# Woven stages of a four-layer convolution network: the frames' shift moved into the statistics, other pauses in the plan, one product per sample in the last layer

## The chip, the cores and the metric

The kernel is one program on one core of a Trainium2 chip. The metric is the time of one execution on the device in microseconds (us). Engines are named as in the profile: PE is TensorE (PEld its loads of weights), DVE is VectorE, ACT is ScalarE, POOL is GpSimd, SP is the engine that issues nearly all DMAs. L584 is line 584 of the kernel.

## The reference

The input x has shape (16, 32, 128, 128), 16 samples b of 32 channels. Four layers follow one another, each of the form x + f(gn(x)), where gn normalises groups of two channels of a sample:

```python
x = x + _L0_conv_ref(_gn(x), ...)   # a row LSTM: scan over 128 columns, two small products per step
x = x + _L1_conv_ref(_gn(x), ...)   # AdderNet: out = -sum over 32 channels and 3x3 taps of |patch - w|
x = x + _L2_conv_ref(_gn(x), ...)   # Hartley transform, 32x32 modes mixed over channels, transform back
x = x + _L3_conv_ref(_gn(x), ...)   # U-net: 5 edge operators, each normalised; 3x3 convs, max-pools,
                                    # 2x2 deconvs; its result multiplies the normalised input
```

The last line is `x + xn * y` with xn the normalised input and y the U-net's output, that is (x - mean) * (1 + istd * y) + mean.

## The kernel before

**Layer 0** (`stage0`, to some 920 us) runs alone; the change does not touch it.

**Layers 1 to 3** are in `rest`. Layer 1 is the class `Differences`. For each of 16 samples and two halves it makes 72 tensors of max(q - w, 0), one per tap and filter group (d_dve on VectorE at L681, 2.36 us; d_act on ScalarE at L678, 7.15 us), and PE sums each with 16 products (L584). Every half ends with `finish` (L567, L569). The quantised input q of the next half is loaded with one DMA of 2145 KB (L553, `q<-q_d`), whose source is read as [4 copies, 32 channels, 66 rows].

Layers 2 and 3 are the class `After`, one generator over groups of four samples. Groups 0, 1 and 2 are woven into layer 1 (the woven stage, to some 6130 us); group 3, and what is left of group 2, run when layer 1 is done (the drain). A group goes through, in this order:

- `forward`: loads xh (L957), products with the transform (L1026, L996), modes exchanged through memory, then `mixing`: 32 rows ky of 16 small products (L1092) with weights `mix` in eight pieces of four rows, three buffers, each piece loaded (L1079) when the piece three before it is used; the result is copied (L1107) and stored.
- `back`: loads zi, products (L1153), then 16 steps n: eight products (L1198) for step n, a pause, and `take_out` of step n - 1 (L1176 adds to the rows xr, L1178 their statistics). Rows are stored (L1182) and the buffer of four is reloaded (L1132) for step n + 4. Then the mean and istd of the group (`bn_aggr` at L1214, `normalised`) go into `stats3`.
- `frames`: loads rows of layer 3's input (L1237) and normalises them on ScalarE (L1248), with scale istd and bias -mean * istd (the shift, `fr_shift`, L1245). They are used by `statistics` (L1288, then es_w at L1348) and by `conv1` (L1603). Between these the weights wf are made from the statistics (L1413, L1415), then the edge sums cut (L1575).
- `small_layers` (L1451, L819), and `last`: per unit and row parity pr, the last composed convolution (L819), s = istd * acc + (1 + istd * bias) (L1730), the multiply (x - mean) * s (L1695), plus mean on ScalarE (L1703), store (L1709).

**The plan.** The order of instructions on each engine is fixed when the program is built, by `Weave`. It keeps planned times for DVE, ACT and PE. After each tap of layer 1, `advance` takes steps of the chain while PE's planned time is less than some 2 us ahead of the time at which the next tap ends. A generator's `yield 1.1` is 1.1 us of PE work; `yield -7.0` is a pause: the chain goes on when the planned time is 7.0 us later; `later(us, step)` puts a step off by so much. A pause puts no wait into the program: it only decides which of layer 1's instructions stand between. The core of it is

```python
elif v < 0:
    wait = -v
...
if wait > 0:
    self.until = self.now + wait
```

In the drain two such generators are stepped in turn, the one with the smaller planned time first. A group starts when its four samples of layer 1 are planned (`("after", 4 * g + 3)`) and the group before has ended.

Of the kernel before, what the change touches and what calls it, by code (L numbers as in the profile page):

```python
# [7 lines left out]
F32 = mybir.dt.float32  # L8
F16 = mybir.dt.float16
I32 = mybir.dt.int32  # L10
AF = mybir.ActivationFunctionType
ALU = mybir.AluOpType
# [3 lines left out]
B, C, H, W = 16, 32, 128, 128  # L16
# [3 lines left out]
M1 = 32  # L20
# [23 lines left out]
def bc_view(t, g):  # L44

    return t.rearrange("b c h w -> (b c) (h w)")[g * 128 : (g + 1) * 128]
# [826 lines left out]
class After:  # L873
# [13 lines left out]
    def work(self, groups):  # L887
        if 0 in groups:
            yield from self.prepare()
        for g in groups:  # L890
            with self.pool("g_sm") as sm:
                yield ("after", 4 * g + 3)
                yield -8.0
                self.stats3 = sm.tile([128, 2, 1], F32, name="stats3")
                yield from self.forward(g)
                with ExitStack() as kept:
                    yield from self.encoder(g, kept)
                    yield from self.last(g)
# [183 lines left out]
    def mixing(self, g, xs, wp, wt):  # L1082


        nc, weave, z_d = self.nc, self.weave, self.d["z"]
        zp = [self.acc() for _ in range(2)]
        zv = [z.rearrange("p (y k b) -> p y k b", k=4, b=8) for z in zp]
        for ky in range(M1):
            w = wt[ky // 4]
            for k in range(16):  # L1090
                j = k // 4
                nc.tensor.matmul(  # L1092
                    zv[ky // 16][32 * j : 32 * j + 32, ky % 16, k % 4, :],
                    w[:, ky % 4, k, :],
                    xs[:, :, k, ky],
                    start=True,
                    stop=True,
                )
            if ky % 4 == 3 and len(wt) < M1 // 4:
                wt.append(self.weights(wp, len(wt)))  # L1100
            yield 1.1
        yield SUMMED
        zs = wp.tile([128, 2, 4, 4, 32], F32, name="zs", bufs=1)
        for half in range(2):
            for y in range(2):
                dst = zs[:, half, :, :, 16 * y : 16 * y + 16].rearrange("p b k y -> p y k b")
                nc.vector.tensor_copy(dst, zv[y][:, :, :, 4 * half : 4 * half + 4])  # L1107
        weave.dve += 2.0
        yield -2.5
        for half in range(2):  # L1110
            for j in range(4):
                first = z_d.offset + 4 * g * 32768 + 512 * half + 128 * j
                dst = bass.AP(z_d.tensor, first, [[1024, 32], [32768, 4], [1, 128]])
                nc.sync.dma_start(dst, zs[32 * j : 32 * j + 32, half].rearrange("p b k y -> p b (k y)"))
        yield -4.0

    def back(self, g, load):


        nc, tc, cst, d, weave = self.nc, self.tc, self.cst, self.d, self.weave  # L1120
        x2, x3, z_d = d["x2"], d["x3"], d["z"]

        with self.pool("t_z") as zp_, self.pool("t_r", 4) as rp:
# [68 lines left out]
            for n in range(16):  # L1192
                s, half = n // 2, n % 2
                pf = [self.acc() for _ in range(2)]
                for i in range(4):
                    for r in range(2):
                        part = slice(64 * half + 32 * r, 64 * half + 32 * r + 32)
                        nc.tensor.matmul(  # L1198
                            pf[r][:, W * i : W * i + W],
                            o1[part, 4 * s + i].rearrange("p b o -> p (b o)"),  # L1200
                            cst["cas_t"][part, :],
                            start=True,
                            stop=True,
                        )
                yield 0.8
                if previous:
                    yield -7.0
                    take_out(*previous)
                previous = n, pf
            yield SUMMED  # L1210
# [2 lines left out]
            mv = zp_.tile([128, 1, 2], F32, name="mv3")  # L1213
            nc.vector.bn_aggr(mv[:, 0, :], stat.rearrange("p a b -> p (a b)"))  # L1214
            yield from normalised(nc, zp_, self.ps, weave, mv, 1, cst["avg2_bc"], 1e-5, self.stats3)

    def frames(self, g, pool):

        nc, x3, weave = self.nc, self.d["x3"], self.weave
        shift = []
        ring = [pool.tile([128, 20, W + 4], F32, name=f"xp{i}") for i in range(2)]
        for t in ring:
            nc.vector.memset(t[:, :, 0], 0.0)
            nc.vector.memset(t[:, :, W + 3], 0.0)

        def parts(ch, half):

            lo, hi = max(16 * ch - 2 + 10 * half, 0), min(16 * ch + 8 + 10 * half, H)
            off = lo - (16 * ch - 2)
            return ring[ch % 2], lo, hi, ring[ch % 2][:, off : off + hi - lo, 2 : W + 2]

        def load(ch, half):
            t, lo, hi, v = parts(ch, half)
            nc.sync.dma_start(v, bc_view(x3, g).rearrange("p (h w) -> p h w", w=W)[:, lo:hi, :])  # L1237

        def normalise(ch, half, us):
            t, lo, hi, v = parts(ch, half)  # L1240

            def step():
                if not shift:
                    shift.append(pool.tile([128, 1], F32, name="fr_shift"))
                    nc.vector.scalar_tensor_tensor(  # L1245
                        shift[0], self.stats3[:, 0], -1.0, self.stats3[:, 1], ALU.mult, ALU.mult
                    )
                nc.scalar.activation(v, v, AF.Identity, bias=shift[0], scale=self.stats3[:, 1])  # L1248
                for edge, r, src, zero in ((lo == 0, 1, 3, 0), (hi == H, 18, 16, 19)):
                    if edge:  # L1250
                        nc.gpsimd.memset(t[:, zero, :], 0.0)
                        nc.scalar.copy(t[:, r, 2 : W + 2], t[:, src, 2 : W + 2])
                own = slice(10 * half, 10 * half + 10)
                nc.scalar.copy(t[:, own, 1], t[:, own, 3])
                nc.scalar.copy(t[:, own, W + 2], t[:, own, W])
                weave.act += 2.0

            return weave.later(us, step)

        chunk = lambda ch: ring[ch % 2]  # L1260
        return load, normalise, chunk

    def statistics(self, g, pool, frames, sides, out, tables):


# [393 lines left out]
    def last(self, g):  # L1659

        nc, tc, cst, weave = self.nc, self.tc, self.cst, self.weave
        with self.pool("l_y") as yp, self.pool("l_x", 2) as xp:
# [18 lines left out]
            p = self.acc()  # L1681
# [4 lines left out]
            mean, istd = ms[:, 0:4], ms[:, 4:8]  # L1686
# [3 lines left out]
            yield -4.0  # L1690

            def multiply(x, s, pr, blk):
                for pc in range(2):
                    v = x[:, blk].rearrange("p (r a w b) -> p r a w b", a=2, b=2, w=64)[:, :, pr, :, pc]
                    nc.vector.scalar_tensor_tensor(v, v, mean[:, blk : blk + 1], s[:, pc], ALU.subtract, ALU.mult)  # L1695
                weave.dve += 1.0


            following = {}
# [16 lines left out]
            def complete(unit):  # L1716
                while following.get(unit):
                    weave.done(following[unit])

            for unit in range(4):  # L1720
                complete(unit - 2)
                x = xr[unit % 2]
                for pr in range(2):
                    acc = [self.acc() for _ in range(4)]
                    for pc in range(2):
                        yield from up.round(y6, 64, acc, lambda j: (2 * pr + pc, 16 * unit + 4 * j, 4, 256 * pc))
                    yield SUMMED
                    for blk in range(4):
                        s = yp.tile([128, 2, 4, 64], F32, name="s", bufs=3)
                        nc.vector.tensor_scalar(  # L1730
                            s.rearrange("p b r w -> p (b r w)"),
                            acc[blk],
                            istd[:, blk : blk + 1],
                            one[:, blk : blk + 1],
                            ALU.mult,
                            ALU.add,
                        )
                        weave.dve += 0.65
                        if blk:
                            multiply(x, previous, pr, blk - 1)  # L1740
                        previous = s
                    multiply(x, previous, pr, 3)
                    yield -2.5
                following[unit] = weave.on_act(lambda x=x, unit=unit: done(x, unit))
            yield -36.0
            for unit in range(4):
                complete(unit)

# [160 lines left out]
```

## Time and profile before

| what | value |
|---|---|
| three timed runs | 7451.15, 7454.95, 7469.55 us (median 7454.95) |
| the profiled execution | span 7432.4 us, TensorE clock granted 0.86 |
| busy over the span | PE 75%, DVE 79%, ACT 71%, POOL 0% |
| d_dve (L681) | 1711 times, 2361 ns each |
| d_act (L678) | 593 times, 7146 ns each |
| last sum of layer 1 (L584) | 6129.4 us |
| group 0: mixing, rows of the way back, last wf, conv1 | from 2268, from 2461, to 2871, from 2903 us |
| group 1: xh, mixing, rows | from 3785, from 3975, from 4162 us |
| group 2: xh, mixing, rows, conv1, end | from 5495, 5689, 5873, 6341, to 7028 us |

The busy shares are means over stages with different limits, so the profile is read by stretches of time. A bracket such as [18.48 <-PE acc L584] at a row of the timeline says how long the engine was idle before it and what released it. A row with a count (x21) merges neighbours of one kind, and its second column is their length together.

### The profile page before, as it was taken

The page shows a single profiled execution, that of the slowest core. Times are in us where ns is not written, and L with a number is a line of the kernel's source. Part 1 is how long each engine was busy: PE and PEld are TensorE (multiplying, and loading weights), DVE is VectorE, ACT ScalarE, POOL GpSimd, SP SyncE. Part 2 cuts the span into 40 slices and gives each one's busy share as a digit, 9 for nine tenths or more (in the row PEclk, how much of TensorE's full clock was granted, in tenths as well). Part 3 has the DMA queues.
Part 4 walks back from the last instruction along what each step waited for, and adds up shares of the span by engine and source line. Part 5 has one row for each costly group of instructions (what it writes and reads, how often), then busy time and mean ns, then how long its engine had stood idle before and what let it go on. Part 6 is the DMA issues. An engine that isn't in the chain of part 4 may idle for free. (4 is left out here: it accounts for less than half of the span.)

```text
span 7432.4 us, 258307 instructions
## 1 busy us (share of the span) xinstructions
PE 5602.5 (75%) x121132; PEld 3087.2 (42%) x121132; DVE 5881.6 (79%) x7180; ACT 5276.7 (71%) x3110; POOL 34.2 (0%) x31
## 2 busy tenths in 40 slices
PE   4888466666676777998777676998777775898897
PEld 3666232222244343333344343333335345554554
DVE  7787599999988989999898988998898994135223
ACT  2556398889987988898898888898887980122222
POOL 0000000000000000000000000000000000000000
PEclk9899788888878888999888887998888885897996
DMA  8655111111033333111433332221343234244314
GB/s 314 225 183 172 61 64 54 46 53 52 33 95 95 119 110 96 57 53 46 98 108 103 102 111 94 63 67 42 75 113 108 82 117 144 65 141 119 80 30 95
DMA packets 374270, 721.68 MB, mean 97 GB/s; under 512 B 50896, under 2 KB 219856, under 8 KB 362320
## 3 DMA queue, kind: packets, MB, share of 16 engines
q1 hardware_dynamic: 372768, 704.58, 31.0%
q8 instruction: 948, 15.53, 0.9%
q14 instruction: 122, 1.00, 0.0%
q10 hardware_dynamic: 432, 0.57, 0.0%
HBM read 507.21 MB, written 164.32 MB: 90 GB/s over the span
## 5 line engine op out<-in xcount | busy, mean ns | idle before, releaser
L678 ACT ACTIVATE d_act<-q,neg 128x8192 f16<-128x8192 f16 (+1 forms) x593 | 4199.2, 7146 | 559.1 <-PE acc L584 512.6
L681 DVE TENSOR_SCALAR d_dve<-q,qw 128x8192 f16<-128x8192 f16 (+1 forms) x1711 | 3941.9, 2361 | 348.3 <-PE acc L584 306.1
L584 PE MATMUL acc<-d_dve,sel 128*32 128x512 f16 x27376 | 1963.3, 416 | 747.7 <-DVE d_dve L681 734.5
L584 PEld LDWEIGHTS <-sel 128*32 128x32 f16 x36864 | 1078.8, 103 | 2405.6 <-issue 1816.9
L1603 PE MATMUL acc<-xp,wf 32*32 32x512 f32 x25600 | 1014.7, 620 | 30.6 <-issue 15.2
L584 PE MATMUL acc<-d_act,sel 128*32 128x512 f16 x9488 | 738.6, 438 | 256.1 <-ACT d_act L678 244.0
L1603 PEld LDWEIGHTS acc<-xp,wf 32*32 32x32 f32 x25600 | 443.5, 105 | 404.4 <-issue 299.4
L1542 ACT ACTIVATE y<-pooled,b 32x128 f32<-32x128 f32 x512 | 204.7, 400 | 519.2 <-DVE pooled L1528 510.4
L819 PE MATMUL acc<-y,u_conv 32*32 32x256 f32 (+1 forms) x9728 | 443.3, 515 | 87.4 <-DVE s L1730 39.5
L207 PE MATMUL pg<-h,wb 64*64 64x20 f32 (+15 forms) x4096 | 403.1, 324 | 95.3 <-DVE h L256 54.1
L207 PE MATMUL pg<-e,wb 64*64 64x20 f32 (+15 forms) x4096 | 360.4, 320 | 16.0 <-DVE e L260 4.3
L244 ACT ACTIVATE gt<-pg,bias 128x20 f32<-128x20 f32 (+15 forms) x1024 | 315.5, 374 | 78.1 <-PE pg L207 70.9
L1248 ACT ACTIVATE xp<-xp,fr_shift,stats 128x1280 f32<-128x1280 f32 (+1 forms) x128 | 182.8, 1434 | 230.1 <-DMA xp<-x_d 174.2
L207 PEld LDWEIGHTS pg<-h,wb 64*64 64x64 f32 x4096 | 251.1, 156 | 131.0 <-DVE h L256 80.7
L819 PEld LDWEIGHTS acc<-y,u_conv 32*32 32x32 f32 x9728 | 199.7, 119 | 252.0 <-issue 155.4
L207 PE MATMUL pg<-xn,wb 64*64 64x28 f32 (+61 forms) x4096 | 291.1, 308 | 10.7 <-ACT gt L244 3.3
L207 PEld LDWEIGHTS pg<-e,wb 64*64 64x64 f32 x4096 | 256.1, 158 | 94.0 <-DVE e L260 65.8
L600 PE MATMUL acc<-q,sel 32*32 32x512 f16 x4608 | 151.8, 532 | 148.1 <-DVE xr L567 99.1
L1703 ACT ACTIVATE xr<-xr,l_ms 128x1024 f32<-128x1024 f32 x64 | 69.9, 1140 | 267.1 <-DVE xr L1695 267.1
L255 ACT ACTIVATE th<-c 128x20 f32<-128x20 f32 (+15 forms) x256 | 81.3, 320 | 239.7 <-DVE c L253 238.2
L1288 PE MATMUL acc<-xp 32*64 32x204 f32 (+3 forms) x8576 | 233.2, 343 | 13.5 <-issue 13.5
L207 PEld LDWEIGHTS pg<-xn,wb 64*64 64x64 f32 x4096 | 222.5, 157 | 35.7 <-ACT gt L244 8.3
(203 smaller groups left out, 4215.5 us busy)
## 6 DMA issues: line engine op xcount, KB each, us to landing
xr<-x_d SPq DMA_DIRECT2D x192, 512.0 KB
xp<-x_d SPq DMA_DIRECT2D x112, 640.0 KB
q<-q_d SPq DMA_DIRECT2D x32, 2145.0 KB
x_d<-xr SPq DMA_DIRECT2D x128, 512.0 KB
x_in<-in_x_dram SPq DMA_DIRECT2D x16, 2048.0 KB
res<-in_x_dram SPq DMA_DIRECT2D x64, 512.0 KB
xn<-in_xs_dram SPq DMA_DIRECT2D x64, 512.0 KB
xn<-xn SPq DMA_DIRECT2D x128, 256.0 KB
```

Source lines behind the costliest of these rows:

```text
L207: nc.tensor.matmul(bank[c][q][64 * pair : 64 * pair + 64, :, :width], wb[half, 4 * kind + KIND[q]].rearrange("p b o -> p (b o)"), v[half], ...
L244: nc.scalar.activation(gt[:, q, :, :n], bank[c][q][:, :, :n], AF.Tanh if q == G else AF.Sigmoid, bias=bias[:, KIND[q] : KIND[q] + 1],)
L255: nc.scalar.activation(th[:, :, :n], cell, AF.Tanh)
L584: self.nc.tensor.matmul(acc[k][32 * j : 32 * j + 32, :], self.sel16[:, i // 9, :], d[:, row : row + 4, c : c + W], start=False, stop=last,)
L600: self.nc.tensor.matmul(acc[k][32 * j : 32 * j + 32, :], self.sel16[rows, 8, :], q[rows, row : row + 4, kw : kw + W], start=tap == 0, stop ...
L678: nc.scalar.activation(dst, src, AF.Relu, bias=self.neg[:, i : i + 1])
L681: nc.vector.tensor_scalar(dst, src, self.qw[:, i : i + 1], 0.0, ALU.subtract, ALU.max)
L819: nc.tensor.matmul(acc[blk][32 * j : 32 * j + 32, o : o + rows * n], t[part, 4 * par + tap, :], src[part, top : top + rows, left : left + ...
L1248: nc.scalar.activation(v, v, AF.Identity, bias=shift[0], scale=self.stats3[:, 1])
L1288: nc.tensor.matmul(gram[blk][j : j + width, at : at + n], xp[part, l, 2 + j : 2 + j + width], xp[part, rows, j : j + width + 4], start=sta ...
L1542: nc.scalar.activation(d, s, AF.Identity, bias=bj)
L1603: nc.tensor.matmul(acc[blk][32 * j : 32 * j + 32, :], tap_of("all", tap)[rows], xp[rows, 4 * j + kh : 4 * j + kh + 4, kw : kw + W], start= ...
```

## The change

It makes the shift once, straight after the statistics of `back`, in a tile of the group, with a pause behind it; the frames then only use it. In `mixing` the planned price of a row is 1.0 instead of 1.1, and after rows 11, 15, 19, 23 and 27 there is a pause of 5.0. The pause before each `take_out` goes from 7.0 to 4.5. In `last` the two multiplies per sample, one for even and one for odd columns, become one over all columns; for it s is written with the two column parities interleaved. The pause at a group's end goes from 36 to 16.

```diff
+                self.shift3 = sm.tile([128, 1], F32, name="shift3")
...
                 wt.append(self.weights(wp, len(wt)))
-            yield 1.1
+            yield 1.0
+            if ky % 4 == 3 and 8 < ky < M1 - 1:
+                yield -5.0
...
                 if previous:
-                    yield -7.0
+                    yield -4.5
                     take_out(*previous)
...
             yield from normalised(nc, zp_, self.ps, weave, mv, 1, cst["avg2_bc"], 1e-5, self.stats3)
+            nc.vector.scalar_tensor_tensor(
+                self.shift3, self.stats3[:, 0], -1.0, self.stats3[:, 1], ALU.mult, ALU.mult
+            )
+            yield -2.5
...
             def step():
-                if not shift:
-                    shift.append(pool.tile([128, 1], F32, name="fr_shift"))
-                    nc.vector.scalar_tensor_tensor(
-                        shift[0], self.stats3[:, 0], -1.0, self.stats3[:, 1], ALU.mult, ALU.mult
-                    )
-                nc.scalar.activation(v, v, AF.Identity, bias=shift[0], scale=self.stats3[:, 1])
+                nc.scalar.activation(v, v, AF.Identity, bias=self.shift3, scale=self.stats3[:, 1])
...
             def multiply(x, s, pr, blk):
-                for pc in range(2):
-                    v = x[:, blk].rearrange("p (r a w b) -> p r a w b", a=2, b=2, w=64)[:, :, pr, :, pc]
-                    nc.vector.scalar_tensor_tensor(v, v, mean[:, blk : blk + 1], s[:, pc], ALU.subtract, ALU.mult)
-                weave.dve += 1.0
+                v = x[:, blk].rearrange("p (r a w) -> p a r w", a=2, w=W)[:, pr]
+                nc.vector.scalar_tensor_tensor(
+                    v, v, mean[:, blk : blk + 1], s.rearrange("p r w b -> p r (w b)"), ALU.subtract, ALU.mult
+                )
+                weave.dve += 0.7
...
-                        s = yp.tile([128, 2, 4, 64], F32, name="s", bufs=3)
+                        s = yp.tile([128, 4, 64, 2], F32, name="s", bufs=3)
                         nc.vector.tensor_scalar(
-                            s.rearrange("p b r w -> p (b r w)"),
-                            acc[blk],
+                            s.rearrange("p r w b -> p b r w"),
+                            acc[blk].rearrange("p (b r w) -> p b r w", b=2, w=64),
...
-            yield -36.0
+            yield -16.0
```

## The prediction

> **What bounds the kernel now.** I read the busy time in stretches first, cut where the last sum of layer 1 stands (6130 us), where group 2's first conv1 product stands (6341) and where group 2 ends (7028):
>
> ```profile
> core 0: us, PE busy (x) PEld busy (x) DVE busy (x) ACT busy (x) POOL busy (x), PEclk, DMA share, GB/s
> 923.00:6130.00 5207.00, 3918.91 (x79458) 1911.08 (x79450) 4788.49 (x3908) 4569.62 (x1245) 26.92 (x16) 0.87 0.27 81
> 6130.00:6341.00 211.00, 116.61 (x2384) 111.35 (x2369) 91.29 (x208) 12.54 (x23) 3.81 (x3) 0.56 0.46 138
> 6341.00:7028.00 687.00, 601.26 (x18232) 367.12 (x18239) 220.91 (x569) 166.54 (x320) 0.88 (x4) 0.88 0.37 101
> 7028.00:7432.00 404.00, 339.54 (x8660) 211.81 (x8645) 103.11 (x279) 92.49 (x169) 0.21 (x1) 0.78 0.28 65
> ```
>
> In the woven stage VectorE is busy 92% and ScalarE 88%: they bound it, and PE has room. In the drain PE bounds it, but for its first 211 us, where PE is busy 55% at a clock of 0.56. There group 2 is in a serial piece (statistics, es_w, wf) while group 3 starts.
>
> Then the idle time. The timeline of single engines has one stall of each kind per group or two:
>
> ```profile
> 2311.82 1.16 PE L1092 MATMUL acc<-xs,mix 128*32 128x8 f32 x29 [21.13 <-DMA mix<-in_mix_dram]
> 2314.89 47.88 DVE L681 TENSOR_SCALAR d_dve<-q,qw 128x8320 f16<-128x8320 f16 x21 [18.48 <-PE acc L584]
> 4018.43 2.39 DVE L681 TENSOR_SCALAR d_dve<-q,qw 128x8320 f16<-128x8320 f16 x1 [15.43 <-PE acc L584]
> 5730.75 2.39 DVE L681 TENSOR_SCALAR d_dve<-q,qw 128x8320 f16<-128x8320 f16 x1 [14.25 <-PE acc L584]
> ...
> 2627.24 1.29 DVE L1176 SCALAR_TENSOR_TENSOR xr<-acc,xr 128x512 f32<-128x512 f32 x2 [14.95 <-issue]
> 4324.92 1.29 DVE L1176 SCALAR_TENSOR_TENSOR xr<-acc,xr 128x512 f32<-128x512 f32 x2 [12.24 <-DMA xr<-x_d]
> ...
> 2647.13 1.25 ACT L1248 ACTIVATE xp<-xp,fr_shift,stats 128x1024 f32<-128x1024 f32 x1 [19.50 <-DVE fr_shift L1245]
> ```
>
> A mixing product waits for its weights, the sums of layer 1 stand behind it on PE, and VectorE runs out of buffers: 18.5 + 15.4 + 14.3 = 48 us. A take_out waits for its reloaded rows: 15.0 + 12.2 = 27 us. SP's timeline tells why:
>
> ```profile
> 2255.45 2.56 SPq L553 DMA_DIRECT2D q<-q_d  x1
> 2274.11 52.43 SPq L1079 DMA_DIRECT2D mix<-in_mix_dram  x5
> ...
> 4284.29 0.55 SPq L553 DMA_DIRECT2D q<-q_d  x1
> 4288.34 0.36 SPq L1132 DMA_DIRECT2D xr<-x_d  x1
> ```
>
> Each time the 2145 KB load of q was issued shortly before. Weights issued at 2274.1 held their product until 2311.8; a reload issued at 4288.3 held its take_out until 4324.9: some 37 us, against a 512 KB reload in about 4 us when nothing is in front (135 GB/s in 2540 to 2544).
>
> Last the chain of waits at the drain's start:
>
> ```profile
> 6135.13 10.78 SPq L957
> 6155.39 8.91 DMA xp<-x_d
> ...
> 6257.83 10.27 DMA xm_d<-xm
> 6269.79 11.39 DMA xw<-xm_d
> ```
>
> Group 2's frames wait behind group 3's loads, then transfers of group 3's forward part; nothing dense is there for PE.
>
> [...] with almost nothing but q moving (5830 to 5855) the DMA share is 0.26, at 105 GB/s. [...] clock 0.51 in 6180 to 6341, where a forward product (L1026) has a median of 401 ns against 277 ns in the woven stage.
>
> **The change, part by part.** A pause is no wait on the chip: it only orders instructions. What it buys is the place of the groups' chain against layer 1. Groups 1 and 2 start (first xh load) at 3785 and 5495, long after their batches are ready, directly when the group before ends. So savings add up.
>
> *Way back, 7.0 to 4.5.* The planner pauses in whole d_dve steps of 2.36 us: three before (7.08), two now (4.72). Take_outs of group 0 go from 2469.6 to 2627.2, less the 15.0 stall 9.5 us each; the new ones come every 7.2. 15 pauses: 34.5 us per group.
>
> *End, 36 to 16.* 16 d_dve steps (37.8) become 7 (16.5): 21 us for groups 0 and 1. The stores forced out are those of ScalarE's last products. The next group's xh loads come earlier on SP; SP already sat 32 us in those (5499.13). Anything queued there is needed later than that except xq (40.6 us of waits in all now): 0 to 15 us lost; I take 0, as the new places fall in mid-half.
>
> *Mixing.* 32 x 0.1 = 3.2 us less, five pauses more. PE stands 3 to 4 us ahead in the plan, so each costs the chain 1 to 2 us, at most 7: 5 us net, 32 at the outside. On PE two or three sums now stand before product 12, which reaches its weights 5 to 7 us later: the stall shrinks by that.
>
> *Shift.* The same 0.15 us VectorE instruction, one d_dve (2.35 us) earlier; the pause costs one step (2.4 us). No DMA moves with it. ScalarE's 19.5 and 16.8 us came from VectorE's own lateness in take_out; group 0's xp loads will now be issued near 2600, behind the q of 2584, and may hold ScalarE as long. I take 0, bounds -15 and +15.
>
> Chain ahead: 34.5 + 21 - 5 - 2.4 = 48 for each of groups 0 and 1, 27 for group 2 (no end): 123 us where layer 1 ends. Group 2 stood 108 us behind its bn_aggr (6022) at 6130; it will stand 231 behind. In group 0 that is 2861, in the last wf (2841 to 2871). So es_w and wf move into the woven stage.
>
> *Stalls of the woven stage.* I put each group against q loads some 165 us apart. Group 0's mixing keeps its place: 18.5 becomes 12. Group 1's starts at 3927 with q at 3961: one late load of weights, 8. Group 2's, near 5600, meets none. Take_outs: group 0's last reload goes out near 2570, ahead of q: 0. Group 1: 3. Group 2's rows now lie over the q of 5822; a reload is issued 10 us after its take_out's start and needed at 29, so 37 - 19 = 18, and 4 for zi behind q. Sum 45 against 75: -30, bounds -70 and +50.
>
> *Moved work.* From group 0's stretch: es_w and es_red 20 x (0.60 + 0.59) = 24 us, wf 16, small ones 7: 47 us of VectorE; nine frames on ScalarE at 1.9: 17. The planner gives taps to whichever engine is free, so 64 / 2 = 32, and 10 for waits like the 5.66 and 9.91 us for gm there: +42, bounds +30 and +80.
>
> *Drain.* Of the 211 us there remain 25 for group 2 (end of wf, cut). Group 3's forward and half of its mixing ran there, 54.5 + 15.0 + 17.3 = 87 us of PE at half clock: 45 us beside conv1. So 211 - 70 = 141 less, of which I give back 30, since group 3's own es_w and wf (6780 to 6863) and its end lose part of their partner: -110, bounds -40 and -150.
>
> *Last layer.*
>
> ```profile
> L1695 DVE SCALAR_TENSOR_TENSOR xr<-xr,l_ms,s 128x256 f32<-128x256 f32 x128 | 55.5, 498 | 8.3 <-DMA out_dram<-xr 7.9 <-DMA xr<-x_d 0.2
> L1730 DVE TENSOR_SCALAR s<-acc,l_ms,l_one 128x512 f32<-128x512 f32 x64 | 50.2, 810 | 171.1 <-PE acc L819 171.1
> L1176 DVE SCALAR_TENSOR_TENSOR xr<-acc,xr x128: 668/683/696, 2469.6 to 6616.2; 128x512 f32<-128x512 f32 x128
> ```
>
> Two products take 2 x 55.5 / 128 = 0.87 us; one of 512 elements 0.65 by L1176 (two in 1.29). 0.2 x 32 = 6 us per group. Groups 0 and 1 give 12 us of VectorE, shared, -6. In groups 2 and 3 two multiplies stand before the last s that PE waits for: 0.4 x 16 = 6, half on the path, -3. The trace has no s written with a step of two: [...]
>
> Sum: -30 + 42 - 110 - 6 - 3 = -107. Against this execution's span 7432.4 gives 7325; the timed runs' median stands 22.5 higher (7454.95): 7348.
>
> **The rivals.** (1) *The head start is swallowed* (chance 0.17): PE is the drain's bound anyway and only idle time goes, 141 becomes about 75 with 20 given back, and the stalls stay at 75: 42 - 55 - 9 = -22 to -45, about 7420. For it: PE busy 601 of 687. Against: the clock of 0.51.
>
> (2) *Collisions with q multiply* (slower, 0.11). Every load of the shortened chain that is issued within some 40 us after q waits 37 us less its slack: in the way back the slack falls from 38 - 13 = 25 to 29 - 10 = 19 us, so each hit costs about 17 on VectorE. Weights, zi, reloads and xp in three groups make twelve places. It decides from 75 + 110 + 9 - 42 = 152 us, nine hits; with twelve, 204 us: 7432 + (204 - 152) gives +52, about 7507. For it: the three groups already hit five. Against: q is in front only a quarter of the time.
>
> (3) *The pauses do not do what they say* (0.06): the planned head start is absorbed, or gain and new waits cancel: within 0.3% (22 us), about what a measurement of this kernel can tell from no change.
>
> **The numbers.** My forecast has 0.66: 7270 to 7400. With (1), of which 0.01 falls within 0.3%, faster by over 0.3% is 0.82, the same 0.07, slower 0.11. The range reaches from 7265 to 7445, leaving out most of (2), half of (3) and a little below.
>
> **What would show it.** Right: group 2's wf before the last L584 and conv1 (L1603) within 40 us after it; take_outs 7.2 us apart; the woven stage 0 to 20 us longer; a drain of about 1190 us in place of 1302; L1026 of group 3 near 280 ns. Wrong: L1176 or L1092 waiting for DMA over 75 us in sum; a drain above 1260; s (L1730) over 0.9 us.

## The result and the profile after

| | before | after |
|---|---|---|
| timed runs, median | 7459.88 us (4 runs) | 7365.85 us (4 runs) |
| lowest and highest | 7451.15, 7469.55 | 7343.01, 7376.03 |
| profiled span | 7432.4 | 7341.2 |

The ratio is 0.9869, with a 95% interval of 0.9843 to 0.9896: the change makes the kernel 94 us faster, where 107 were forecast. Both profiled executions lie about as far below their medians (7434.2 us by 26, 7343.0 by 23), so their spans may be compared: 91 us less. In the lines of after, L584, L678, L681, L819 and L1695 keep their numbers; L1026 is now L1027, L1092 is L1093, L1176 is L1179, L1245 is L1219, L1248 is L1249, L1348 is L1349, L1415 is L1416, L1603 is L1604 and L1730 is L1732.

First the busy time in stretches, cut at the same four events as before (last sum, group 2's first conv1 product, end of group 2; the columns are start, end, length, busy time and number of PE, PEld, DVE, ACT and POOL, the clock, DMA share and GB/s):

```profile
924.00:6097.00 5173.00, 3907.64 (x80210) 1900.11 (x80194) 4789.52 (x3859) 4551.91 (x1258) 61.69 (x17) 0.87 0.28 82
6097.00:6249.00 152.00, 81.62 (x1080) 79.52 (x1078) 82.34 (x184) 3.56 (x6) 3.60 (x2) 0.52 0.47 142
6249.00:6914.00 665.00, 577.57 (x18054) 358.53 (x18056) 214.05 (x543) 160.10 (x311) 0.88 (x4) 0.90 0.40 111
6914.00:7341.00 427.00, 360.16 (x9378) 229.40 (x9353) 104.75 (x255) 98.83 (x179) 0.21 (x1) 0.80 0.27 63
```

The woven stage ends at 6097 in place of 6130, so it is 33 us shorter. Its VectorE is as busy as before (4789.5 against 4788.5 us): what went is idle time. By cause its waits changed so: for reloaded rows at the take_outs 27 us less, for gm at es_w 16 less, for PE at d_dve 11 less (306.1 to 295.0), for xh 16 more; the rest are small. The first stretch of the drain is 152 us in place of 211, 59 us less, still at half clock (0.52). The other two together take 1092 us, as before (687 + 404 = 1091). So the 91 us are 33 + 59 less 1, and nothing came from conv1 on.

The stalls of the woven stage, from the timelines of VectorE and ScalarE:

```profile
2325.60 4.62 DVE L681 TENSOR_SCALAR d_dve<-q,qw 128x8192 f16<-128x8192 f16 x2 [14.10 <-PE acc L584]
4020.24 2.35 DVE L681 TENSOR_SCALAR d_dve<-q,qw 128x8192 f16<-128x8192 f16 x1 [15.66 <-PE acc L584]
5702.32 4.65 DVE L681 TENSOR_SCALAR d_dve<-q,qw 128x8192 f16<-128x8192 f16 x2 [18.29 <-PE acc L584]
...
2580.59 0.16 DVE L1219 SCALAR_TENSOR_TENSOR shift<-stats 128x1 f32<-128x1 f32 x1
...
2596.47 1.24 ACT L1249 ACTIVATE xp<-xp,shift,stats 128x1024 f32<-128x1024 f32 x1
```

The three stalls behind the mixing weights are there still: 14.1 + 15.7 + 18.3 = 48 us, as before. ScalarE's first frame no longer waits for the shift: the shift was made at 2580.6, the frame runs at 2596.5 and shows no bracket. Before, 19.5 us stood there. In the whole woven stage no frame waits for the shift any more (36.3 us before); in the drain group 3's first frame still does, 24.4 us (11.0 before). ScalarE's idle time fell by less than the 36, some 17 us: it now waits longer for xq (45 us in place of 26) and, in the last layer, for the product (L1695, 25 us in place of none).

The groups of the woven stage show what became of the take_outs' waits, and a new one before the normalisation of xh:

```profile
L1179 DVE SCALAR_TENSOR_TENSOR xr<-acc,xr 128x512 f32<-128x512 f32 x96 | 61.3, 677 | 0.0
L980 DVE TENSOR_TENSOR xh<-xh,mr 128x2048 f32<-128x2048 f32 x24 | 54.8, 2284 | 23.5 <-DMA xh<-x_d 23.5
```

The last number before the arrow is idle time: 0.0 at the take_outs (27.2 before), 23.5 at xh (7.5 before). SP's timeline gives the reason:

```profile
4245.00 0.36 SPq L1135 DMA_DIRECT2D xr<-x_d  x1
4283.88 0.56 SPq L553 DMA_DIRECT2D q<-q_d  x1
...
5793.10 2.12 SPq L553 DMA_DIRECT2D q<-q_d  x1
5840.61 0.36 SPq L1135 DMA_DIRECT2D xr<-x_d  x1
```

With a take_out every 6.9 us (9.2 to 9.5 before) a group's twelve reloads fit between two loads of q: the last one of group 1 is issued 39 us ahead of q, the first one of group 2 is issued 48 us behind it.

The chain of waits at the drain's start (start, length, what):

```profile
6114.64 15.01 DMA gm<-in_gram_dram x2
...
6133.41 13.86 PE acc L1027 x64
...
6215.66 10.09 DMA xw<-xm_d
```

Group 2's frames, which waited there behind group 3's loads, are done; but its es_w (with gm), group 3's forward products and the exchange of modes still stand in a row between the last sum and conv1 at 6249.

### The profile page after: what moved, and what is told of

Read it like the earlier page. It is cut to its first block, busy times and chain, and to the rows that moved or that the text cites. A ratio compares the mean times of both kernels' runs of the same rounds, so it can differ in the third digit from the quotient of the medians.

```text
span 7341.2 us, 258222 instructions
## 1 busy us (share of the span) xinstructions
PE 5543.0 (76%) x121132; PEld 3046.4 (41%) x121132; DVE 5867.6 (80%) x7056; ACT 5250.5 (72%) x3106; POOL 68.8 (1%) x31
## 5 line engine op out<-in xcount | busy, mean ns | idle before, releaser
L678 ACT ACTIVATE d_act<-q,neg 128x8192 f16<-128x8192 f16 (+1 forms) x589 | 4171.4, 7149 | 549.1 <-PE acc L584 498.4
L681 DVE TENSOR_SCALAR d_dve<-q,qw 128x8192 f16<-128x8192 f16 (+1 forms) x1715 | 3949.3, 2358 | 338.8 <-PE acc L584 295.0
L584 PE MATMUL acc<-d_dve,sel 128*32 128x512 f16 x27440 | 1943.7, 413 | 662.7 <-DVE d_dve L681 655.2
L584 PEld LDWEIGHTS <-sel 128*32 128x32 f16 x36864 | 1072.7, 103 | 2331.0 <-issue 1727.7
L1604 PE MATMUL acc<-xp,wf 32*32 32x512 f32 x25600 | 1011.7, 619 | 18.4 <-issue 8.7
L584 PE MATMUL acc<-d_act,sel 128*32 128x512 f16 x9424 | 724.1, 432 | 283.5 <-ACT d_act L678 275.1
L1604 PEld LDWEIGHTS acc<-xp,wf 32*32 32x32 f32 x25600 | 440.6, 104 | 383.5 <-issue 282.2
L819 PE MATMUL acc<-y,u_conv 32*32 32x256 f32 (+1 forms) x9728 | 435.6, 508 | 83.6 <-issue 41.0
L819 PEld LDWEIGHTS acc<-y,u_conv 32*32 32x32 f32 x9728 | 201.9, 118 | 245.1 <-issue 150.5
L207 PEld LDWEIGHTS pg<-e,wb 64*64 64x64 f32 x4096 | 251.8, 156 | 92.2 <-DVE e L260 62.9
L1640 DVE TENSOR_TENSOR acc<-acc,cut 128x4 f32<-128x4 f32 x256 | 35.2, 164 | 307.9 <-PE acc L1604 305.6
L1249 ACT ACTIVATE xp<-xp,shift,stats 128x1280 f32<-128x1280 f32 (+1 forms) x128 | 182.4, 1434 | 131.8 <-DMA xp<-x_d 106.7
```

The lines of the kernel that those rows point to most:

```text
L207: nc.tensor.matmul(bank[c][q][64 * pair : 64 * pair + 64, :, :width], wb[half, 4 * kind + KIND[q]].rearrange("p b o -> p (b o)"), v[half], ...
L584: self.nc.tensor.matmul(acc[k][32 * j : 32 * j + 32, :], self.sel16[:, i // 9, :], d[:, row : row + 4, c : c + W], start=False, stop=last,)
L678: nc.scalar.activation(dst, src, AF.Relu, bias=self.neg[:, i : i + 1])
L681: nc.vector.tensor_scalar(dst, src, self.qw[:, i : i + 1], 0.0, ALU.subtract, ALU.max)
L819: nc.tensor.matmul(acc[blk][32 * j : 32 * j + 32, o : o + rows * n], t[part, 4 * par + tap, :], src[part, top : top + rows, left : left + ...
L1249: nc.scalar.activation(v, v, AF.Identity, bias=self.shift3, scale=self.stats3[:, 1])
```

## The experiments

After the result I held this theory: a pause only fixes where the chain stands among the taps of layer 1, so the effect of a part depends on what else is there, and parts do not add. The rival is the forecast's: each part has its own price. In the expectations, theory A is the forecast, theory C is that the early shift matters because the way back has become short, and theory D that mixing's pauses matter in group 3, in the drain. B, E and F are told where they are tested. All kernels compute the whole output. Ratios are to the kernel before on the same chip; where a kernel is compared with kernel 11, the difference of the ratios is multiplied by 7452 us and is uncertain by some 17 to 20 us (both intervals together).

| kernel | ratio [95%] | median us |
|---|---|---|
| 1 way back alone | 0.9975 [0.9961, 0.9989] | 7416.1 |
| 2 end alone | 1.0019 [1.0009, 1.0028] | 7438.4 |
| 3 mixing alone | 1.0017 [1.0009, 1.0025] | 7440.6 |
| 4 last layer alone | 0.9997 [0.9986, 1.0008] | 7429.6 |
| 5 after, old shift | 0.9917 [0.9904, 0.9930] | 7386.3 |
| 6 after, old mixing | 0.9959 [0.9947, 0.9971] | 7419.8 |
| 7 after, old last layer | 0.9955 [0.9937, 0.9973] | 7424.6 |
| 8 after, q in four DMAs | 0.9852 [0.9838, 0.9866] | 7343.4 |
| 9 after, mixing's pauses in group 3 alone | 0.9929 [0.9912, 0.9946] | 7399.8 |
| 10 after, in groups 0 to 2 alone | 0.9918 [0.9900, 0.9936] | 7396.2 |
| 11 after, again | 0.9867 [0.9848, 0.9886] | 7350.2 |
| 12 as 8, rows in four DMAs too | 0.9827 [0.9809, 0.9846] | 7321.2 |

The kernel before had medians of 7430.2 (1 to 4), 7451.8 (5 to 8) and 7452.4 us (9 to 12).

**1. The shorter way back alone**

```diff
-                    yield -7.0
+                    yield -4.5
```

> Only the pause in the way back goes from 7.0 to 4.5. Theory A (the forecast): each group gains 34.5 us of head start and they add up, so at group 2's bn_aggr the chain is some 45 taps of layer 1 (100 us) further ahead than before, and the time falls by 60 to 80 us. Theory B (from the trace after): what groups 0 and 1 gain is lost again before their ends, only group 2's own 16 to 20 taps arrive; the time falls by 27 us of take_out stalls and some 35 us of drain, 50 to 70 us. The two differ in the taps, not much in the time. In both the take_out waits for DMA (15.0 and 12.2 us) should be gone.

It gives 7430.2 x 0.0025 = 19 us. The reloads behind q were gone, as in after. A place is told in taps, by how many of layer 1's 2304 tensors had been begun. Group 2's statistics stood 19 taps earlier (at tap 2234 in place of 2253), as theory B had it and not the 45 of theory A, and the drain's first stretch fell from 211 to 150 us. But from conv1 on the drain took 1142 us, 51 more, and the woven stage ended at 6127.8, only 2 us earlier. Both theories had the time wrong (60 to 80 and 50 to 70 us). ScalarE, from its timeline and VectorE's, in group 0:

```profile
2586.10 2.46 DVE L569 BATCH_NORM_STATS2 stat<-xr 128x6 f32<-128x512 f32 x4
2592.71 2.35 DVE L681 TENSOR_SCALAR d_dve<-q,qw 128x8192 f16<-128x8192 f16 x1 [4.15 <-PE acc L584]
2594.98 0.15 DVE L1245 SCALAR_TENSOR_TENSOR fr_shift<-stats 128x1 f32<-128x1 f32 x1
2595.22 1.26 ACT L1248 ACTIVATE xp<-xp,fr_shift,stats 128x1024 f32<-128x1024 f32 x1 [21.28 <-DVE fr_shift L1245]
2613.10 2.35 DVE L681 TENSOR_SCALAR d_dve<-q,qw 128x8192 f16<-128x8192 f16 x1 [7.96 <-PE acc L584]
```

The end of a half (L569 here) came to lie between the statistics and the shift. The first frame on ScalarE waits for the shift 21.3 us, and ScalarE's taps of layer 1 stand behind it; VectorE then waits 8 us for PE, which lacks ScalarE's tensors. It was so in all three groups (64.4 us of ScalarE, against 36.3 in two groups before).

**2. The shorter end alone**

```diff
-            yield -36.0
+            yield -16.0
```

> Only the pause at a group's end goes from 36 to 16. Theory A: 21 us of head start for each of groups 0 and 1, 42 us at group 2, the drain shorter by about as much: 25 to 40 us faster. Theory B: the head start does not live to group 2's statistics: within 15 us of before, group 2's bn_aggr at most 6 taps earlier.

It is slower by 0.19%, where theory A had it 25 to 40 us faster. Group 2's mixing came 6 taps earlier, but its take_outs and statistics at taps 2193 and 2253, exactly as before, which is theory B: the head start was gone within the group. What it left were longer waits of PE for the weights, 67.0 us against 55.7 in the woven stage.

**3. Mixing's pauses alone**

```diff
-            yield 1.1
+            yield 1.0
+            if ky % 4 == 3 and 8 < ky < M1 - 1:
+                yield -5.0
```

> Only mixing's rows at 1.0 and its five pauses. Theory A: the stalls at the weights shrink by what the pause delays the product, 48 us in sum to about 30: some 10 us faster at most. Theory B: the weights still land behind the load of q and the sums held back are only others: stalls stay near 48 us, time within 15 us of before.

It is slower by 0.17%, although PE's wait for weights fell to 37.8 us: the shrinking that I forecast is there, on PE, when mixing is changed alone. VectorE's three stalls behind it fell only from 48 to 42 us (14.7 + 11.6 + 16.2), so theory B came nearer, in the stalls and in the time. Statistics stayed at tap 2253, a reload behind q still cost 12.3 us, and the woven stage ended at 6132.5.

**4. One product per sample alone**

```diff
-                for pc in range(2):
-                    v = x[:, blk].rearrange("p (r a w b) -> p r a w b", a=2, b=2, w=64)[:, :, pr, :, pc]
-                    nc.vector.scalar_tensor_tensor(v, v, mean[:, blk : blk + 1], s[:, pc], ALU.subtract, ALU.mult)
+                v = x[:, blk].rearrange("p (r a w) -> p a r w", a=2, w=W)[:, pr]
+                nc.vector.scalar_tensor_tensor(
+                    v, v, mean[:, blk : blk + 1], s.rearrange("p r w b -> p r (w b)"), ALU.subtract, ALU.mult
+                )
```

> Only the last layer's one multiply per sample. Theory A: 9 us faster (6 in the woven stage, 3 in the drain). Theory B: the multiply takes 0.72 us where two took 0.87, so 10 us of VectorE for two groups in the woven stage, half of it shared with ScalarE: 5 to 8 us, not to be told from none.

No difference that can be told: 2 us less, with -10 to +6 in the interval. The instruction is cheaper, as its group in after shows:

```profile
L1695 DVE SCALAR_TENSOR_TENSOR xr<-xr,l_ms,s 128x512 f32<-128x512 f32 x128 | 91.9, 741 | 7.1 <-DMA out_dram<-xr 7.0
```

Before, the products were 256 of 491 ns, 110.3 us: 18 us less VectorE in all, about half of it in the woven stage. Writing s with a step of two costs nothing (L1732 takes 814 ns, L1730 took 809).

**5. After, with the shift made in the frames again**

```diff
-            nc.vector.scalar_tensor_tensor(
-                self.shift3, self.stats3[:, 0], -1.0, self.stats3[:, 1], ALU.mult, ALU.mult
-            )
-            yield -2.5
...
+                if not shift:
+                    shift.append(pool.tile([128, 1], F32, name="fr_shift"))
...
+                nc.scalar.activation(v, v, AF.Identity, bias=shift[0], scale=self.stats3[:, 1])
```

> The changed kernel with the shift made in the frames again and without its pause of 2.5. Theory A (the forecast): the shift is worth nothing, the ratio to before stays near 0.987. Theory C (from the run with the way back alone, where ScalarE sat 21.3, 21.2 and 21.9 us for the shift, made behind a half's finish, and VectorE then 8.0, 8.3 and 7.9 us): with the shorter way back the statistics end at the turn of a half, and the shift before the finish is what turns the gain to account: the woven stage is 20 to 30 us longer than in the changed kernel, ratio 0.990 to 0.992, with those three ScalarE waits back.

The loss is (0.9917 - 0.9867) x 7452 = 37 us against kernel 11. Theory C's waits in the woven stage are back:

```profile
DVE d_dve L681 <- PE acc L584: 321.1, 117, 16.4
ACT xp L1250 <- DVE fr_shift L1247: 60.1, 3, 21.9
```

VectorE waits 17 to 26 us longer for PE than in the two profiles of after (304.4 and 295.0), ScalarE 60.1 us for the shift. But the woven stage ends only 14 us later than in kernel 11 (6117.6 against 6103.6), where theory C had 20 to 30. The other 23 us lie in the drain from conv1 on (1115 against 1092 us), and that share is not explained by this wait. The shift's place and the pause behind it were taken out together; which of the two counts is not shown.

**6. After, with mixing as before**

```diff
-            yield 1.0
-            if ky % 4 == 3 and 8 < ky < M1 - 1:
-                yield -5.0
+            yield 1.1
```

> The changed kernel with mixing at 1.1 a row and without its five pauses. Theory A: the pauses take a few us off the stalls at the weights: 5 to 15 us slower than the changed kernel, ratio 0.988 to 0.989. Theory D: in the drain, mixing's pauses set which of group 3's steps stand beside group 2's conv1, and the 50 us by which the drain from conv1 on is shorter in the changed kernel (1092) than with the way back alone (1142) come from them: ratio 0.993 to 0.996. If it is neither, at most 5 us.

It loses (0.9959 - 0.9867) x 7452 = 69 us, though the same part alone loses 13. Of it 15 lie in the woven stage, 10 in the drain's first stretch (163 us) and 44 from conv1 on (1136).

**7. After, with two products per sample** (the reverse of the diff at 4)

> The changed kernel with two multiplies per sample and s in two planes again. Theory A: 9 us slower than the changed kernel (VectorE's time), ratio 0.988. Theory E: the planned 1.0 against 0.7 us per sample shifts group 2's last layer against group 3 in the drain, and the 50 us of drain from conv1 on come from that: ratio 0.993 to 0.996.

It loses 66 us by the ratios; its profiled execution is the fastest of its seven (7386.0), so its lengths are those of a good run. In this one kernel the head start did add up: group 1's xh loads began at tap 1293 (1311 in after), group 2's statistics at tap 2198, 55 taps or 124 us earlier than before. The stretches of busy time ahead of the last sum and from conv1 on:

```profile
924.00:6183.00 5259.00, 3971.96 (x80622) 1933.95 (x80614) 4830.95 (x4005) 4579.53 (x1267) 54.83 (x17) 0.87 0.27 82
...
6191.00:7384.00 1193.00, 1022.60 (x27738) 634.86 (x27733) 364.99 (x940) 258.62 (x489) 4.68 (x7) 0.82 0.36 96
```

Conv1 of group 2 starts 8 us after the last sum and the drain takes 1201 us: the forecast's -110 in the drain is met with -101. But the woven stage is 86 us longer than in after: VectorE has 41 us more work there (es_w, es_red and wf are 39 of it; the second product adds 10, and six d_dve fewer take 13 off) and 45 us more idle time, where the chain waits for its own transfers, as at the exchange of modes:

```profile
DVE xw L1065 <- DMA xw<-xm_d: 23.5, 5, 5.9
```

So half of what the full head start gives in the drain is lost in the woven stage: -101 against +53 over the kernel before, and the median of the timed runs stands a further 38 us above the profiled one. The loss is of the size of theory E's, but not at its place: it lies in the woven stage, and the drain as a whole is 43 us shorter than in after.

**8. After, with q loaded by four DMAs of 32 partitions**

```diff
-        self.nc.sync.dma_start(q, bass.AP(q_d.tensor, first, [[0, 4], [(H + 2) * P, C], [1, (self.R + 2) * P]]))
+        for j in range(4):
+            self.nc.sync.dma_start(
+                q[32 * j : 32 * j + 32], bass.AP(q_d.tensor, first, [[(H + 2) * P, C], [1, (self.R + 2) * P]])
+            )
```

> The changed kernel with the load of q issued as four DMAs, one for each copy of 32 partitions[...]. If the stalls at the weights come from parts of them waiting behind q on few DMA engines, [...] the three stalls of 14.1, 15.7 and 18.3 us of VectorE fall under 5 each: 30 to 45 us faster than the changed kernel, ratio near 0.981 to 0.983. If the weights are late for another reason (their own issue, or bandwidth in all), the stalls stay and the time is the changed kernel's.

The transfers over 40 us at group 0's mixing, first of after (2270 to 2310, q issued at 2271.7), then of this kernel (2255 to 2295, q issued at 2258.4); each figure is the busy share of the 16 DMA engines in 1 us, in tenths:

```profile
DMA  1069972337699963328889963221498998932123
```

```profile
DMA  1103899959999999779930008795006599000000
```

After q is issued, the engines are now mostly 9 tenths busy (2258 to 2275; 189 to 257 GB/s from 2264 to 2270) and then free; in after they are at 2 to 3 tenths where nothing but q moves (68 to 69 GB/s from 2276 to 2279). PE's waits for mixing's weights in the woven stage are gone (47.3 us in after), and with them the three stalls of VectorE, as expected. The stage ends at 6083.5, 20 us ahead of kernel 11. But these 20 us are won at its start, where all of layer 1 waits for the first load of q (VectorE's waits, first in kernel 11, then here):

```profile
DVE d_dve L681 <- DMA q<-q_d: 38.9, 1, 38.9
```

```profile
DVE d_dve L684 <- DMA q<-q_d: 17.0, 1, 17.0
```

The first sum stands at 899.4 in place of 922.5, and from the first sum to the last the stage takes 5184 us, in kernel 11 5181. VectorE's waits for PE at d_dve are 307.4 us in all, against 304.4: what went at the weights came back in other places, so that by these two profiles the waits for weights were worth nothing by themselves. From conv1 on the drain took 1116 us. The whole gains 11 us by the ratios (0.9852 against 0.9867), within the intervals, where 30 to 45 were expected.

**9. After, with mixing's pauses in group 3 alone**

```diff
-            yield 1.0
-            if ky % 4 == 3 and 8 < ky < M1 - 1:
+            yield 1.0 if g == 3 else 1.1
+            if ky % 4 == 3 and 8 < ky < M1 - 1 and g == 3:
```

> The changed kernel with mixing's price of 1.0 and its pauses in group 3 alone, which runs in the drain; groups 0 to 2 as before. Theory D (the pauses' gain is in the drain, where they set what of group 3 stands beside group 2): from group 2's conv1 to the end as in the changed kernel, 1090 to 1115 us against 1136 without any pauses; the woven stage some 10 to 20 us longer by the stalls at the weights; 10 to 25 us slower than the changed kernel. Theory F (the pauses' gain is in the woven stage, by where they leave group 2): as without any, some 65 us slower than the changed kernel.

It is 46 us slower than kernel 11 by the ratios, between theory D's 10 to 25 and theory F's 65: neither holds by itself. I expected the woven stage to be longer without the pauses there, and it was not: it ended at 6097. This profiled execution was the fastest of six, 17 us under their median, so this miss may be the run's. The drain's first stretch was 163 us, as in kernel 6, and 1121 followed.

**10. After, with them in groups 0 to 2 alone** (the same edit with `g < 3`)

> The counterpart: pauses in groups 0 to 2, none in group 3. Theory D: the woven stage is the changed kernel's to the instruction (last sum near 6097), the drain from conv1 on 1130 to 1145 us: 30 to 50 us slower than the changed kernel. Theory F: as the changed kernel within 10 us.

It is 38 us slower than kernel 11 by the ratios. Woven stage and first stretch are those of after (6102 and 153 us); from conv1 on it takes 1144 us, 52 more. That is theory D's place and size. Of the 52, 34 lie in group 2's conv1 (6255 to 6611 us, against 6257 to 6579 in kernel 11). The busy time in a part of it (same columns), and PE's timeline just ahead of that part:

```profile
6335.00:6375.00 40.00, 37.66 (x737) 18.02 (x752) 2.14 (x12) 7.64 (x17) 0.21 (x1) 0.52 0.23 77
```

```profile
6331.15 3.64 PE L1093 MATMUL acc<-xs,mix 128*32 128x8 f32 x176
6337.34 1.75 PE L1093 MATMUL acc<-xs,mix 128*32 128x8 f32 x48 [2.56 <-issue]
```

For 40 us PE is busy 94% at a granted clock of 0.52, and does 737 products. Kernel 11 at the same place:

```profile
6337.00:6377.00 40.00, 38.60 (x1258) 22.56 (x1228) 2.74 (x12) 4.90 (x10) 0.00 (x0) 1.00 0.19 55
```

1258 products at full clock (1.00): 40 x (1 - 737 / 1258), by this estimate some 17 us of the 34, are this. Ahead of the half clock stands a run of 176 of mixing's small products and a gap of 2.6 us. The same is seen in the two other kernels with the way back shortened and no pauses in group 3's mixing, kernel 6 (24 us at 0.51, after 143 products and 2.68 us) and kernel 1 (41 us at 0.50, after 178 products and 2.60 us).

In after the pauses cut mixing into pieces between which conv1's products stand, and beside mixing the clock is at half (0.50) for at most 7 us at a time (6324 to 6330). That the run and the gap bring the half clock is an inference from where they stand; no run tried it by itself. They are not needed for it: kernel 7 has such a spell in group 2's conv1 with no product of mixing ahead, and PE was not idle for more than 1.1 us at a time in the 40 us before it:

```profile
6230.00:6260.00 30.00, 30.00 (x299) 18.31 (x298) 11.19 (x19) 9.96 (x22) 0.00 (x0) 0.50 0.59 154
```

**11. After, again**

> The changed kernel once more, on the chip of these runs, as the one to compare with: ratio to before near 0.987. Its profile also tells how far the drain's length moves from run to run in the same order of instructions.

On another chip it gives the same ratio (0.9867 against 0.9869). The first stretch of the drain is 153 us and the rest 1092, as in the first profile (152 and 1092). Two profiles that agree to 1 us make it unlikely that the differences of 20 to 50 us in the drain named above are scatter of the runs; each of the other kernels has one profile only.

**12. As 8, with the rows for q, the rows of layer 1 and their stores in four DMAs too**

```diff
+def jc_parts(t, b, half, at=0, rows=16):
+    first = t.offset + b * CHW + (64 * half + at) * W
+    return [bass.AP(t.tensor, first + 16 * W * j, [[HW, C], [1, rows * W]]) for j in range(4)]
...
-        self.nc.sync.dma_start(t, jc_rows(self.d["x1"], b, i // 2, 8 * (i % 2), 8))
+        for j, v in enumerate(jc_parts(self.d["x1"], b, i // 2, 8 * (i % 2), 8)):
+            self.nc.sync.dma_start(t[32 * j : 32 * j + 32], v)
...
```

> The changed kernel with q loaded by four DMAs, and layer 1's other loads and stores (xq, xr, x2)[...] in four DMAs each. If few DMA engines are the trouble there as well, ScalarE's waits for xq (59.0 us in the changed kernel) fall under 25 and the time is 10 to 25 us under the changed kernel's, ratio 0.980 to 0.985. If SP's four times as many issues delay what is queued behind them, it gives back what the load of q brought: ratio 0.985 to 0.990.

7316 to 7337 us, against 7344 to 7376 for kernel 11 on the same chip: 29 us faster, and the fastest version here, ahead of both kernels.

All of it lies in the woven stage, which ends at 6047.3, 56 us earlier than in kernel 11; from conv1 on 23 are given back (1116 against 1092). Of the 56, 29 come at the start again (first sum at 893.8 in place of 922.5), and 28 between the first sum and the last (5153.5 against 5181.1 us). ScalarE's waits for xq fell from 62.9 to 12.5 us, as expected, and VectorE's for xh from 19.1 to none.

## Why the prediction was right, and where it was not

The sum was nearly right, its terms were not: two errors, of -39 and +55 us, cancelled for the most part, and that is luck. By its own steps, on the profiled spans:

| term | forecast | measured |
|---|---|---|
| stalls and moved work, woven stage, with its part of the last layer | -30 + 42 - 6 = +6 | -33 |
| drain, with its part of the last layer | -110 - 3 | -58 |
| sum | -107 | -91 |

**"So savings add up" failed.** 123 us of head start were to reach group 2's statistics; they stood at tap 2229 in place of 2253. That is 24 taps of 2.25 us (5173 us by 2304 taps), or 54 us, and near what the drain's first stretch lost (59). That the way back's head start is what shortens this stretch shows over all kernels: it is 212 to 214 us with the old way back (before, 2, 3, 4) and 148 to 163 with the new one (8 in kernel 7). Taps alone do not give its length: kernel 1, with 19 of them, lost 62 us there. Counting by taps shows where the rest went:

| event | before, tap | after, tap |
|---|---|---|
| group 0 statistics (`bn_aggr`) | 814 | 794 |
| its conv1 begins, ends | 927, 1153 | 910, 1138 |
| its last row | 1292 | 1293 |
| group 1 `bn_aggr` | 1534 | 1514 |
| its last row | 2012 | 2010 |
| group 2 mixing begins | 2102 | 2096 |
| its `bn_aggr` | 2253 | 2229 |

Each group gains 20 taps in its way back and has lost them when it ends; only the last woven group's own gain, and some taps of its beginning, reach the drain. Kernel 2 shows the same for the end's pause by itself. In group 0, after and kernel 7 are alike up to the first s of the last layer: 15 taps ahead of before where conv1 ends, 6 at that s (1223 against 1229). At the last row kernel 7, whose planned price per product is the old one, is 11 ahead (1281 against 1292), after no longer. These 12 taps go to the part with one product per sample; alone, in kernel 4, it moved the last row by 6 taps the same way (1298 against 1292). A second place is the turn between two halves of layer 1: in kernel 2 group 1's products with zi begin at tap 1430 in place of 1436, but their copies at 1447 as before, and what follows stands where it stood; a half begins at 1440. That this turn holds the chain I only argue from the plan. So it hangs on the plan's details and not on a law.

**Moved work: the condition did not come.** The +42 was for es_w and wf moving into the woven stage. They did not move (es_w at 6103 to 6144, wf at 6198 to 6222). Where they did, in kernel 7, the stage took 86 us more than in after: 41 of work (es_w, es_red and wf 39 of it, where 40 were worked out) and 45 of waits, where I took 10; and I had halved the work, since ScalarE would share it. So the forecast's own case is worth less than what came: kernel 7's span is 48 us below that of before, after's 91.

**Stalls: the halves were swapped.** The take_outs were to keep 21 us and kept 0: I put group 2's rows over a load of q, but with 6.9 us per take_out the twelve reloads fit between two of them in every group. The weights were to keep 20 and kept 48: when kernel 3 changes mixing alone, PE's wait does shrink (55.7 to 37.8 us, VectorE's stalls from 48 to 42), in after only to 47.3. The q loads moved as well: in group 2, where I expected no collision, q was issued at 5645.7 and the weights from 5651.5. In sum 48 + 0 against 75 is -27, and the forecast had -30. This nearness is luck too: the sum had no term for xh, which took 16 us more, nor for gm at es_w, which took 16 less. And in kernel 8's profile, without the three stalls at the weights, the stage was not shorter between its first sum and its last: a stall's length is no price.

**Shift: 0 was wrong, outside its bounds.** "I take 0, bounds -15 and +15" priced it against the kernel before. With the other parts in place, its absence and that of its pause cost 37 us (kernel 5). The wait which it removes is made longer by another part of the same change (kernel 1), and that I had not looked for.

**Mixing: 5 us lost forecast, 69 us worth in the whole.** I counted it only in the woven stage. What its pauses do in the drain, where they let conv1 stand between mixing's products, I had not priced at all: taking them out of group 3 alone costs 38 us (kernel 10), out of groups 0 to 2 alone 46 (kernel 9).

**Last layer: the prices were near.** By busy time one product takes 0.72 us (91.9 by 128) in place of 0.86 (110.3 by 128), which saves 0.14 where 0.2 were forecast, and the step of two costs nothing (814 ns against 809). By itself it gives nothing that can be told from zero; in the whole it counts through the plan (kernel 7), which is again a matter of order.

**Rivals.** Rival (1), the head start swallowed by PE's bound, has a part: the gain in the drain was 58 us against its 55. But the reason is another: what did not arrive was the head start itself, not PE's room. Rival (2) did not come: weights and take_outs together waited 47 us in after. It does show where it was not looked for, as the 12.2 us at xh, the longest of its waits. Rival (3), the head start absorbed, names what became of 69 of the 123 us, though not its total. Of the five signs of being right only one came, the take_outs (6.9 us apart): wf stayed behind the last sum, conv1 began 152 us after it, the woven stage was 33 us shorter and not longer, the drain is 1244 us, and the clock of group 3's forward products stayed at half (0.52 in that stretch, a median of 401 ns); the stretch kept its serial piece, with PE busy 54%. Of the signs of being wrong none came.

**The load of q.** In before, with almost nothing but q moving, the DMA share was 0.26 at 105 GB/s (5830 to 5855). With four loads of 32 partitions in place of one (kernel 8) the engines are busy 9 tenths while q passes, at 189 to 257 GB/s, and weights issued behind it no longer hold a product (47.3 us in after, none in kernel 8; in kernel 12 no such wait of over 2.7 us). That few engines were at work before, as the expectations put it, is my reading of the share: which engines carried q was not shown, and the number of loads and the shape of each were changed together.

**What stays open.** The single parts, counted alone, sum to about +6 us (-19 + 14 + 13 - 2), the whole gives -94 to -99. That the parts work together is shown by taking one out of the whole: shift, mixing and last layer then count 37, 69 and 66 us. No pair was tried by itself. Of the 52 us between kernels 10 and 11 some 17 are the half clock in the spell shown; the other 35, and the 22 to 28 that kernels 5, 8, 9 and 12 lose from conv1 on, I did not resolve (part may be the clock again: from conv1 on its mean is 0.83 in kernel 10 and 0.86 in kernel 11). The change without its shorter end, and the shift alone, were not tried.

## What to carry to other kernels

Where the order of instructions is fixed by a plan, count positions in units of the dominant work (here taps), before and after: this shows at once whether time won in one place is still there in the next, and here single edits were worth between 0.25% faster and 0.19% slower and together 1.3% faster. Price a part with the other parts in place: here a shorter pause lengthened exactly the wait that another part removes. Here a load of 2145 KB, which moved at 105 GB/s with a DMA share of 0.26, held up what was issued behind it: weights issued 19 us after it (2274.1 in before) let their product start only at 2311.8, 38 us later. Cutting it into four loads of 32 partitions took away 47 us of waits for weights, and that alone shortened nothing between the first sum and the last; it paid 23 us at the start, where nothing can go on before the load is there. Done for the rows as well, it made the best version. So ask of a wait what else stands ready to take its place.

## What the runs showed of the hardware that I had not expected

PE ran at half clock (0.52) for 40 us while busy 94% (kernel 10), for 41 us at 0.50 and busy 93% in kernel 1 and for 24 at 0.51 and busy 99% in kernel 6, each time after a gap of 2.6 to 2.7 us behind a run of products of 128x8; in kernel 7 for 30 us at 0.50 while busy throughout, after no gap above 1.1 us. In kernel 11, at the place of kernel 10's spell, the clock was 1.00 with PE busy 97%. In before the clock was 0.51 over 161 us in which PE was busy 59% (6180 to 6341). In these runs a high busy share did not secure the full clock. What brought it down is not shown.
